# Layer 1 of a four-layer graph network: rows of the neighbours scaled ahead of the loop, GpSimd's product over both chunks of a pair in one instruction, and the last rows stored through three queues

## The chip, the cores and the metric

The kernel runs on one core of a Trainium2 chip. Its time is device microseconds (us) of one execution; the time before is 559.01 us, the median of three runs from 558.31 to 559.95 us. A core has five engines that run their own instruction streams in order and wait for each other through semaphores: TensorE (PE in the profile, with its weight loads as PEld), VectorE (DVE), ScalarE (ACT), GpSimd (POOL) and SyncE (SP), which here only starts transfers. SP, ACT and POOL can start DMA transfers.

## The reference, cut to what matters

Four graph layers, each followed by a residual and a layer norm, work on x (3327 nodes by 64 features) and one dense matrix adj (3327 by 3327). The change is in layer 1, a hyperbolic attention layer, and in the stores of the last layer.

```python
x_tan = _logmap0(x, C)
left = x_tan @ att_W[:D] + att_b
right = x_tan @ att_W[D:]
adj_att = jax.nn.sigmoid(left + right.T) * adj
x_local = _logmap(x[:, None, :], x[None, :, :], C)
support_t = jnp.einsum('ij,ijd->id', adj_att, x_local)
return _proj(_expmap(x, support_t, C), C)
...
x = _layernorm(x + _L1_gnn_ref(x, adj, L1_gnn_att_W, L1_gnn_att_b), axis=-1)
```

For every pair of nodes (i, j) layer 1 needs a sigmoid times adj, and a logarithmic map of the two points. After the layer norm of layer 0 all rows have nearly the same norm, and the kernel replaces the map's scalar factor by a cubic polynomial in one inner product of i and j. The cubic is evaluated as a linear (real) factor times a quadratic factor.

## The kernel before

Nodes are padded to 3328 = 26 blocks of 128. In layer 1 (`near_sphere`) the 128 partitions hold neighbours j of one block, and the free axis holds nodes i. The work is cut into 104 tiles `(cp, jb, ci)`: two column halves cp, 26 blocks jb, and two chunks ci. A tile is 128 partitions by 2 x 416 = 832 elements. Two tiles with the same cp and jb form a pair (here pair k has the tiles 2k and 2k + 1); they share one slab of adj and one sigmoid of 1664 elements.

For a tile t the program issues:

- `products(t)` (L1099), PE: the inner products of j and i into a PSUM tile pq; three such tiles exist, so the products of t + 3 wait for the last reader of t.
- `attention(k)` (L1065 to L1088), once for a pair: SP loads adj, ACT computes sg = sigmoid(lb + rb) over 1664 elements (L1075), and GpSimd multiplies it by adj, u = sg * at (L1086), in two instructions of 832 elements, one for each tile. There are two buffers of sg and four of u. For pair 0 the sigmoid is cut in two as well.
- `linear(t)` (L1105): DVE computes a = (pq + dl) * u (L1111), where dl is one number for each partition j, and then ACT squares in place, pq = (gas * pq + al)^2 (L1112).
- `gather(t)` (L1116): DVE computes v = (pq + constant) * a (L1120), and PE adds xv(j)^T v to the accumulators (L1132).

All engines of this stage follow an order written out by hand (`manual_schedule`). The loop over t is `linear(t + 1)`, `gather(t)`, and, at even t, `attention(t // 2 + 2)` and, in the first half, `rows_of_sums` (L1226, a small ACT instruction). From this follow the orders on the engines:

- DVE: a(t+1), v(t), a(t+2), v(t+1), ...
- ACT: for t = 2k: square(t+1), sigmoid of pair k + 2, rows_of_sums, square(t+2), square(t+3), ...
- POOL: u(0), u(1), u(2), ...

At t = 13 and t = 25 PE also turns two more groups of blocks, and ACT copies them out of PSUM ahead of its next sigmoid.

Ahead of the loop DVE writes the rows of i into ri (`rows_of_i`, L1218; these rows carry -2 * gas) and the last columns of ri and xv, GpSimd computes dl and al (L1255 to L1257), and PE turns ri and lj. lj holds rows of j: 63 differences of features and in the last column (aa + 1) * inv_s (L1007). Here s is the layer norm's scale of a row, inv_s its inverse, ga another number of a row, and gas = ga * s.

After the loop, `near_end` works on 128 x 26 statistics (k, gp, ps and so on, L1464 to L1568), rebuilds the layer's output with `x2 = alpha * m + beta * xc` and the like, and layer 2 begins at L419.

The last layer's second half ends in `last_out`. DVE scales three parts of the output, in the order blocks 10 to 12, 6 to 9, 0 to 5, and each part is stored when it is ready. Block 12 has only 127 real rows, which go by themselves through ACT's queue (L848); the others go through SP (10 and 11), ACT (6 to 9) and SP (0 to 5).

Of the kernel before, what the change touches and what calls it, by code (L numbers as in the profile page):

```python
# [10 lines left out]
F32 = mybir.dt.float32  # L11
# [49 lines left out]
CUBIC_ROOT = -1.39229596292  # L61
CUBIC_SHIFT = 0.0453813261445
CUBIC_REST = 1.75705840270866
NEIGH = 100
# [10 lines left out]
def kernel(  # L75
# [234 lines left out]
    def layers(ctx, x2, x3, begun_here, kept, ready, ahead_ctx, strm):  # L310
# [496 lines left out]
        def last_out(h, accT):  # L807
# [33 lines left out]

            for s, queue in zip(parts[::-1], (nc.sync, nc.scalar, nc.sync)):
                nc.vector.scalar_tensor_tensor(
                    hh[:, s], hh[:, s], -0.5, spread(r[:, s], s.stop - s.start),
                    op0=ALU.mult, op1=ALU.mult,
                )
                if s.stop == NBH:
                    nc.scalar.dma_start(out[N - rows :], hh[:rows, NBH - 1])  # L848
                store(queue, h, hh, s)
# [45 lines left out]
    with tc.tile_pool(name="l1", bufs=1) as l1:  # L895
# [20 lines left out]
        with tc.tile_pool(name="l1a", bufs=1) as l1a, tc.tile_pool(  # L916
# [86 lines left out]
            vec(ga, vq[:, 1], rq[:, 1], ALU.mult)  # L1003
            stt(inv_s, vq[:, 1], -0.5 / 0.9, r2[:, 1], op0=ALU.mult, op1=ALU.mult)
            sca(aa, g1, -1.0, 1.0, ALU.mult, ALU.add)
            vec(gas, ga, s, ALU.mult)
            stt(lj[:, :, D - 1], aa, 1.0, inv_s, op0=ALU.add, op1=ALU.mult)  # L1007
        in_order.close()

        def near_sphere(mT, ljT_0, xm, sq_e, t_e, rows_63):  # L1010
# [3 lines left out]
            with tc.tile_pool(name="n1", bufs=1, reuse_waits="tile") as n1, tc.tile_pool(  # L1014
# [50 lines left out]
                def attention(pair):  # L1065

                    if pair >= len(tiles) // 2:
                        return
                    cp, jb, _ = tiles[2 * pair]
                    at, sl = load(cp, jb), slot(jb)  # L1070
                    sg = n1w.tile([P, 2, 2 * CW], F32, tag="sg", name=f"sg_{pair}")
                    lbs = lbh[:, :, cp * 2 * CW : (cp + 1) * 2 * CW]

                    def sigmoid(of):
                        nc.scalar.activation(  # L1075
                            sg[:, :, of], lbs[:, :, of], AF.Sigmoid, bias=rb[:, sl : sl + 1]
                        )

                    chunks = (slice(0, CW), slice(CW, 2 * CW))
                    if pair:  # L1080
                        sigmoid(slice(0, 2 * CW))
                    for ci, of in enumerate(chunks):
                        if not pair:
                            sigmoid(of)
                        u = n1w.tile(TW, F32, tag="u", bufs=4, name=f"u_{pair}_{ci}")
                        nc.gpsimd.tensor_tensor(u, sg[:, :, of], at[:, :, of], ALU.mult)  # L1086
                        us[2 * pair + ci] = u
                        yield  # L1088
# [16 lines left out]
                def linear(t):  # L1105

                    if t >= len(tiles):
                        return
                    one = slice(slot(tiles[t][1]), slot(tiles[t][1]) + 1)
                    a_s[t] = n1w.tile(TW, F32, tag="a", bufs=3, name=f"a_{t}")  # L1110
                    stt(a_s[t], pqs[t], dl[:, one], us.pop(t), op0=ALU.add, op1=ALU.mult)  # L1111
                    nc.scalar.activation(  # L1112
                        pqs[t], pqs[t], AF.Square, bias=al[:, one], scale=gas[:, one]
                    )
# [109 lines left out]
                def rows_of_sums(jb):  # L1224
                    sl = slot(jb)
                    nc.scalar.activation(  # L1226
                        xv[:, sl, : D - 1], xc[:, sl, : D - 1], AF.Copy, scale=xf[:, sl : sl + 1]
                    )
# [12 lines left out]
                with tc.manual_schedule(  # L1241
# [6 lines left out]
                    keep((NB - 3, NB - 4))  # L1248
                    stt(xf, gas, CUBIC_LEAD / -256.0, gas, op0=ALU.mult, op1=ALU.mult)
                    nc.vector.tensor_copy(ri[:, :, D - 1], ga)  # L1250
                    vec(xv[:, :, D - 1], lj[:, :, D - 1], xf, ALU.mult)
                    rows_of_i(0, 4)
                    rows_of_i(4, NBH)

                    nc.gpsimd.tensor_scalar(dl, g1, CUBIC_ROOT, -1.0, ALU.mult, ALU.add)  # L1255
                    nc.gpsimd.tensor_tensor(dl, dl, inv_s, ALU.mult)
                    nc.gpsimd.tensor_scalar(al, ga, -1.0, CUBIC_SHIFT, ALU.mult, ALU.add)  # L1257
                    spread_a, spread_b = bank(0, left, 0, 4), bank(1, left, 13, 4)
# [30 lines left out]
                    for t in range(len(tiles)):  # L1289
# [13 lines left out]
                        if t == len(tiles) - 4:  # L1303
                            of = slice(0, 2 * CW)
                            nc.gpsimd.tensor_tensor(xm[:, of], mT[:, of], ljT[0][:, of], ALU.mult)
# [3 lines left out]
                            gp.tensor_tensor(gk, gs, ga, ALU.mult)  # L1309
# [14 lines left out]
                        if t == len(tiles) - 2:  # L1324
# [5 lines left out]
                                t_e.rearrange("p (a k h) -> p a k h", a=2, k=3), pm[..., P:]  # L1330
                            )
                    stt(rxn, r2[:, 0], -0.5, inv_s, op0=ALU.mult, op1=ALU.mult)
                    vec(xn, aa, rxn, ALU.mult)

        def near_end(mT, ljT, xm, sq_e, t_e, rows_63, x2):
# [4 lines left out]
            with tc.tile_pool(name="l1e", bufs=1) as l1e, tc.tile_pool(  # L1340
# [78 lines left out]

                gt, q, k, ps = st("gt"), st("q"), st("k"), st("ps")  # L1420
                gp = st("gp")
# [42 lines left out]
                vec(k, p, gks, mul)  # L1464
                vec(gp, p, gss, mul)
                vec(k, k, gt, add)
                vec(ps, p, s, mul)

# [49 lines left out]
                vec(be, be, ck, sub)  # L1518
                alp = of(mul, al, ps, "alp")
                al2 = of(mul, al, al, "al2")  # L1520
# [45 lines left out]
                alpha, beta = dl, xf  # L1566
                stt(alpha, n_r, -0.5, al, op0=mul, op1=mul)
                stt(beta, n_r, -0.5, be, op0=mul, op1=mul)  # L1568

                for b, g, n in ((0, 0, 1), (0, 1, 3), (3, 12, 1), (1, 4, 4), (2, 8, 4)):  # L1570
# [4 lines left out]
                    vec(lj[:, sl], lj[:, sl], one(beta, sl), mul)  # L1575
                    vec(lj[:, sl], lj[:, sl], pt, add)

                for g, n in threes:
                    sl = slots(g, n)
                    vec(x2[:, sl], x2[:, sl], one(alpha, sl), mul)  # L1580
                    vec(xc[:, sl], xc[:, sl], one(beta, sl), mul)
                    vec(x2[:, sl], x2[:, sl], xc[:, sl], add)
# [270 lines left out]
```

## Time and profile before

| what | us |
|---|---|
| median of three runs | 559.01 |
| the profiled execution | 559.12 |
| its span, from the first to the last instruction | 557.4 |
| from the first a (L1111) to the end of the last v (L1120) of layer 1 | 22.22 to 227.68 |
| layer 2's first matmul (L419) | 243.0 |
| the last DVE instruction ends | 550.1 |
| busy: PE, DVE, ACT, POOL | 525.1, 377.8, 276.2, 215.5 |

The profile is of one execution. Its span runs from the first to the last instruction. The timeline gives for each instruction the start and the duration in us, the engine, the line of the kernel, the output and inputs by their names, and in brackets the idle time in front of it with what ended it. Consecutive instructions of the same line are merged with their number behind an x. DVE and ACT start an instruction a little before the one ahead of it has ended, so the step from start to start is shorter than a duration.

```profile
PE   7889989999999999999999999999999999999991
PEld 5522222222222222764444444444455555545541
DVE  6899999999999999899000010300578877887733
ACT  4799999999999998530000100000364333433321
POOL 3699999999999999300000000000001000000000
PEclk9899999999999999899999999999999999999996
DMA  8977776766676717799999039999019994799601
```

These are the busy tenths of 40 equal slices of 13.9 us. In the slices from 22 to 220 us, layer 1's loop, four engines are busy nearly all of the time.

### The profile page before, as it was taken

The page shows a single profiled execution, that of the slowest core. Times are in us where ns is not written, and L with a number is a line of the kernel's source. Part 1 is how long each engine was busy: PE and PEld are TensorE (multiplying, and loading weights), DVE is VectorE, ACT ScalarE, POOL GpSimd, SP SyncE. Part 2 cuts the span into 40 slices and gives each one's busy share as a digit, 9 for nine tenths or more (in the row PEclk, how much of TensorE's full clock was granted, in tenths as well). Part 3 has the DMA queues.
Part 4 walks back from the last instruction along what each step waited for, and adds up shares of the span by engine and source line. Part 5 has one row for each costly group of instructions (what it writes and reads, how often), then busy time and mean ns, then how long its engine had stood idle before and what let it go on. Part 6 is the DMA issues. An engine that isn't in the chain of part 4 may idle for free.

```text
span 557.4 us, 7490 instructions
## 1 busy us (share of the span) xinstructions
PE 525.1 (94%) x2841; PEld 226.5 (41%) x2841; DVE 377.8 (68%) x547; ACT 276.2 (50%) x323; POOL 215.5 (39%) x138
## 2 busy tenths in 40 slices
PE   7889989999999999999999999999999999999991
PEld 5522222222222222764444444444455555545541
DVE  6899999999999999899000010300578877887733
ACT  4799999999999998530000100000364333433321
POOL 3699999999999999300000000000001000000000
PEclk9899999999999999899999999999999999999996
DMA  8977776766676717799999039999019994799601
GB/s 287 357 254 232 209 229 201 224 210 227 206 237 211 220 60 272 294 427 425 422 423 418 16 141 422 420 426 413 15 55 328 342 327 177 244 270 362 257 1 37
DMA packets 33893, 143.57 MB, mean 258 GB/s; under 512 B 10269, under 2 KB 11959, under 8 KB 28855
## 3 DMA queue, kind: packets, MB, share of 16 engines
q1 hardware_dynamic: 31511, 142.40, 69.9%
q10 hardware_dynamic: 2336, 0.59, 0.5%
q8 instruction: 24, 0.39, 0.3%
q14 instruction: 22, 0.18, 0.1%
HBM read 141.53 MB, written 0.87 MB: 255 GB/s over the span
## 4 chain that ended last, share of the span: by engine, by line
PE 66%; DVE 20%; ACT 8%; issue 3%; DMA 1%; DVEq 0%
PE cnt L419 25%; PE pq L1099 12%; DVE v L1120 12%; PE cnt L524 11%; PE acc L720 6%; ACT sg L1075 4%; PE acc L735 3%; ACT pq L1112 3%; DVE a L1111 2%; DVE w L537 1%; PE cnt L410 1%; DVE mask L339 1%; DMA x<-in_x 1%; PE x_w L1435 1%; PE pn_l L371 1%
## 5 line engine op out<-in xcount | busy, mean ns | idle before, releaser
L1086 POOL TENSOR_TENSOR u<-sg,at 128x832 f32<-128x832 f32 x88 | 169.9, 1959 | 3.5 <-ACT sg L1075 3.1
L1099 PE MATMUL pq<-riT,ljT 64*128 64x416 f32 x416 | 100.2, 560 | 15.2 <-DVE v L1120 6.2
L1111 DVE SCALAR_TENSOR_TENSOR a<-pq,dl,u 128x832 f32<-128x832 f32 x104 | 112.1, 1078 | 2.9 <-PE pq L1099 2.8
L1112 ACT ACTIVATE pq<-pq,al,gas 128x832 f32<-128x832 f32 x104 | 105.0, 1011 | 15.2 <-DVE a L1111 14.3
L1120 DVE SCALAR_TENSOR_TENSOR v<-pq,a 128x832 f32<-128x832 f32 x104 | 105.8, 1017 | 1.1 <-ACT pq L1112 0.7
L1132 PE MATMUL acc<-v,xv 128*64 128x416 f32 x416 | 95.4, 537 | 0.1
L1075 ACT ACTIVATE sg<-lb,rb 128x1664 f32<-128x1664 f32 (+1 forms) x53 | 87.3, 1647 | 0.1
L539 ACT ACTIVATE w<-cnt 128x832 int16<-128x832 f32 x55 | 47.2, 863 | 71.5 <-PE cnt L524 71.4
L419 PE MATMUL cnt<-at_l,lj 128*64 128x416 f32 x448 | 80.2, 513 | 0.0
L651 POOL TENSOR_TENSOR s<-sq,s 128x384 bf16<-128x384 f32 (+1 forms) x4 | 4.1, 1026 | 195.0 <-ACT s L650 195.0
L504 ACT ACTIVATE x<-cnt 128x416 f32<-128x416 f32 x8 | 4.1, 517 | 130.6 <-PE cnt L419 130.6
L1099 PEld LDWEIGHTS pq<-riT,ljT 64*128 64x128 f32 x416 | 31.5, 184 | 88.3 <-DVE v L1120 83.0
L537 DVE TENSOR_SCALAR w<-cnt 128x832 int16<-128x832 f32 x49 | 50.2, 1024 | 25.2 <-PE cnt L524 23.8
L524 PE MATMUL cnt<-mask,tri 128*128 128x416 bf16 x208 | 53.5, 339 | 0.1
L720 PE MATMUL acc<-w,s 128*128 128x416 bf16 x208 | 52.6, 339 | 0.5 <-DVE hid L792 0.5
L524 PE MATMUL cnt<-mask,rest 128*128 128x416 bf16 x200 | 51.6, 340 | 1.2 <-ACT w L539 0.6
L419 PEld LDWEIGHTS cnt<-at_l,lj 128*64 128x64 f32 x448 | 31.9, 137 | 46.0 <-issue 45.2
L1132 PEld LDWEIGHTS acc<-v,xv 128*64 128x64 f32 x416 | 20.6, 134 | 61.0 <-issue 57.8
L339 DVE TENSOR_SCALAR mask<-ah 128x1664 bf16<-128x1664 f32 x42 | 43.4, 1034 | 0.5 <-DMA ah<-in_adjT 0.5
L407 DVE COPY lj<-pn_l 128x512 f32<-128x512 f32 (+1 forms) x4 | 2.4, 592 | 60.9 <-PE pn_l L371 60.9
L419 PE MATMUL cnt<-kept,lj 128*64 128x416 f32 x224 | 41.2, 513 | 0.0
L1086 POOL TENSOR_TENSOR u<-sg,kept 128x832 f32<-128x832 f32 x16 | 31.0, 1959 | 3.6 <-ACT sg L1075 3.6
(286 smaller groups left out, 411.7 us busy)
## 6 DMA issues: line engine op xcount, KB each, us to landing
at_l<-in_adjT SPq DMA_DIRECT2D x24, 1664.0 KB, 13.2
at<-in_adjT SPq DMA_DIRECT2D x44, 832.0 KB, 5.0
ah<-in_adjT SPq DMA_DIRECT2D x42, 832.0 KB, 6.5
bt_l<-in_adjT SPq DMA_DIRECT2D x8, 1664.0 KB, 16.8
kept<-in_adjT SPq DMA_DIRECT2D x7, 1664.0 KB, 9.2
lb<-lf_rows SPq DMA_DIRECT2D x2, 384.0 KB, 4.3
ljT<-ljT SPq DMA_DIRECT2D x4, 128.0 KB, 5.2
x<-in_x ACTq DMA_DIRECT2D x1, 416.0 KB, 5.3
```

The lines of the kernel that those rows point to most:

```text
L339: nc.vector.tensor_scalar(mask[q], at, 0.0, None, ALU.not_equal)
L419: nc.tensor.matmul(acc[c][h * D : (h + 1) * D, :], hw[:, slot(jb), :], blocks[jb][:, o : o + CW], start=c not in begun, stop=last, skip_gr ...
L524: nc.tensor.matmul(cnt[c][:, e, :], mat, mask[q][:, of], start=start, stop=(mat is tri), skip_group_check=True,)
L537: nc.vector.tensor_scalar(w.bitcast(I16), cnt[c], 0.0, None, ALU.max)
L720: nc.tensor.matmul(acc[h, c][:, e, :], s12[:, slot(jb)].rearrange("p t d -> p (t d)"), ws[q, c][:, e, :], start=first, stop=last,)
L1075: nc.scalar.activation(sg[:, :, of], lbs[:, :, of], AF.Sigmoid, bias=rb[:, sl : sl + 1])
L1086: nc.gpsimd.tensor_tensor(u, sg[:, :, of], at[:, :, of], ALU.mult)
L1099: nc.tensor.matmul(pq[:, h, :], ljT[h != jb // NBH][rows, of], riT[rows, ch * CW : (ch + 1) * CW], start=True, stop=True,)
L1111: stt(a_s[t], pqs[t], dl[:, one], us.pop(t), op0=ALU.add, op1=ALU.mult)
L1112: nc.scalar.activation(pqs[t], pqs[t], AF.Square, bias=al[:, one], scale=gas[:, one])
L1120: stt(w, pqs.pop(t), CUBIC_REST, a_s.pop(t), op0=ALU.add, op1=ALU.mult)
L1132: nc.tensor.matmul(accs[cp, ci][h * D : (h + 1) * D, :], xv[:, slot(jb), :], w[:, h, :], start=(jb == orders[cp][0]), stop=(jb == orders[c ...
```

## The change

Three edits are made.

1. lj's 63 features and its last column are scaled by s, so that pq comes out scaled by s of its row j. The last column becomes aa + 1, the real factor's shift becomes the same constant for all j (`CUBIC_PLUS`), an immediate in L1111 in place of the column dl, and the square's scale becomes ga. The scaling is done ahead of the loop by three DVE multiplications (`scaled`), `rows_of_i` is cut into three instead of two, dl is no longer computed, inv_s is computed behind the loop, and some 128 x 26 statistics of `near_end` change or fall away.
2. The product sg * adj is written in place over sg, of which there are three buffers now; the four buffers of u fall away. For pairs 0 and 1 it is still made in two instructions; from pair 2 on, one instruction covers the 1664 elements of both chunks.
3. In `last_out` the 127 rows of block 12 are split into 112, through ACT's queue, and 15, through POOL's; blocks 6 to 9 go through SP and blocks 0 to 5 through ACT.

The order of instructions on PE and ACT is the same as before, the operands and the stores aside.

```diff
+CUBIC_PLUS = 2 * CUBIC_ROOT - 1
...
-            for s, queue in zip(parts[::-1], (nc.sync, nc.scalar, nc.sync)):
+            most = rows // 16 * 16
+            for s, queue in zip(parts[::-1], (nc.sync, nc.sync, nc.scalar)):
...
                 if s.stop == NBH:
-                    nc.scalar.dma_start(out[N - rows :], hh[:rows, NBH - 1])
+                    nc.scalar.dma_start(out[N - rows : N - rows + most], hh[:most, NBH - 1])
+                    nc.gpsimd.dma_start(out[N - rows + most :], hh[most:rows, NBH - 1])
                 store(queue, h, hh, s)
...
-            stt(inv_s, vq[:, 1], -0.5 / 0.9, r2[:, 1], op0=ALU.mult, op1=ALU.mult)
...
-            stt(lj[:, :, D - 1], aa, 1.0, inv_s, op0=ALU.add, op1=ALU.mult)
+            sca(lj[:, :, D - 1], aa, 1.0, None, ALU.add)
...
-                    sg = n1w.tile([P, 2, 2 * CW], F32, tag="sg", name=f"sg_{pair}")
+                    sg = n1w.tile([P, 2, 2 * CW], F32, tag="sg", bufs=3, name=f"sg_{pair}")
...
-                    for ci, of in enumerate(chunks):
+
+                    wide = slice(0, 2 * CW)
+                    for of in chunks if pair < 2 else (wide,):
                         if not pair:
                             sigmoid(of)
-                        u = n1w.tile(TW, F32, tag="u", bufs=4, name=f"u_{pair}_{ci}")
-                        nc.gpsimd.tensor_tensor(u, sg[:, :, of], at[:, :, of], ALU.mult)
-                        us[2 * pair + ci] = u
+                        nc.gpsimd.tensor_tensor(sg[:, :, of], sg[:, :, of], at[:, :, of], ALU.mult)
+                        for ci, c in enumerate(chunks):
+                            if of in (c, wide):
+                                us[2 * pair + ci] = sg[:, :, c]
                         yield
...
-                    stt(a_s[t], pqs[t], dl[:, one], us.pop(t), op0=ALU.add, op1=ALU.mult)
+                    stt(a_s[t], pqs[t], CUBIC_PLUS, us.pop(t), op0=ALU.add, op1=ALU.mult)
                     nc.scalar.activation(
-                        pqs[t], pqs[t], AF.Square, bias=al[:, one], scale=gas[:, one]
+                        pqs[t], pqs[t], AF.Square, bias=al[:, one], scale=ga[:, one]
                     )
...
-                    stt(xf, gas, CUBIC_LEAD / -256.0, gas, op0=ALU.mult, op1=ALU.mult)
-                    nc.vector.tensor_copy(ri[:, :, D - 1], ga)
+                    def scaled(b, n):
+
+                        sl = slice(2 * b, 2 * (b + n))
+                        vec(
+                            lj[:, sl, : D - 1], lj[:, sl, : D - 1],
+                            s[:, sl].unsqueeze(2).to_broadcast([P, 2 * n, D - 1]), ALU.mult,
+                        )
+
+                    scaled(9, 4)
+                    sca(ri[:, :, D - 1], ga, -CUBIC_ROOT, None, ALU.add)
+                    rows_of_i(0, 4)
+                    stt(xf, ga, CUBIC_LEAD / -256.0, ga, op0=ALU.mult, op1=ALU.mult)
                     vec(xv[:, :, D - 1], lj[:, :, D - 1], xf, ALU.mult)
-                    rows_of_i(0, 4)
-                    rows_of_i(4, NBH)
-
-                    nc.gpsimd.tensor_scalar(dl, g1, CUBIC_ROOT, -1.0, ALU.mult, ALU.add)
-                    nc.gpsimd.tensor_tensor(dl, dl, inv_s, ALU.mult)
-                    nc.gpsimd.tensor_scalar(al, ga, -1.0, CUBIC_SHIFT, ALU.mult, ALU.add)
+                    vec(gss, xf, s, ALU.mult)
+                    rows_of_i(4, 8)
+                    scaled(5, 4)
+                    rows_of_i(8, NBH)
+                    scaled(0, 5)
+
+                    nc.gpsimd.tensor_scalar(
+                        al, ga, CUBIC_PLUS, CUBIC_SHIFT - CUBIC_ROOT, ALU.mult, ALU.add
+                    )
...
-                            gp.tensor_tensor(gss, gs, s, ALU.mult)
-                            gp.tensor_tensor(gks, gk, s, ALU.mult)
-                            gp.tensor_scalar(gks, gks, -2.0, None, ALU.mult)
+                            gp.tensor_scalar(gks, gk, -2.0, None, ALU.mult)
...
+                    stt(inv_s, vq[:, 1], -0.5 / 0.9, r2[:, 1], op0=ALU.mult, op1=ALU.mult)
                     stt(rxn, r2[:, 0], -0.5, inv_s, op0=ALU.mult, op1=ALU.mult)
...
-                vec(ps, p, s, mul)
...
-                vec(be, be, s, mul)
...
+                vec(beta_c, beta, s, mul)
```

More of the change, by code (lines that the diff above doesn't have):

```diff
@@ L1226, in rows_of_sums @@
                     nc.scalar.activation(
-                        xv[:, sl, : D - 1], xc[:, sl, : D - 1], AF.Copy, scale=xf[:, sl : sl + 1]
+                        xv[:, sl, : D - 1], xc[:, sl, : D - 1], AF.Copy, scale=gss[:, sl : sl + 1]
                     )
@@ L1418, in p_of @@
                         )
-                gt, q, k, ps = st("gt"), st("q"), st("k"), st("ps")
+                gt, q, k = st("gt"), st("q"), st("k")
                 gp = st("gp")
@@ L1464, in near_end @@
                 vec(k, p, gks, mul)
-                vec(gp, p, gss, mul)
+                vec(gp, p, gs, mul)
                 vec(k, k, gt, add)
-                vec(ps, p, s, mul)
                 first = in_bank("first_w")
@@ L1518, in near_end @@
                 vec(be, be, ck, sub)
-                alp = of(mul, al, ps, "alp")
+                alp = of(mul, al, p, "alp")
                 al2 = of(mul, al, al, "al2")
@@ L1565, in near_end @@
                 stt(n_r, n_r, -3.0, t, op0=add, op1=mul)
-                alpha, beta = dl, xf
+                alpha, beta, beta_c = dl, xf, gss
                 stt(alpha, n_r, -0.5, al, op0=mul, op1=mul)
@@ L1580, in near_end @@
                     vec(x2[:, sl], x2[:, sl], one(alpha, sl), mul)
-                    vec(xc[:, sl], xc[:, sl], one(beta, sl), mul)
+                    vec(xc[:, sl], xc[:, sl], one(beta_c, sl), mul)
                     vec(x2[:, sl], x2[:, sl], xc[:, sl], add)
```

## The prediction

> **What bounds the kernel now.** I read the 40 slices first, then the busy time of each engine in two stretches of layer 1's loop (columns: window and length, then for PE, PEld, DVE, ACT and POOL the busy us and the number of instructions, then clock, DMA share and GB/s):
>
> ```profile
> 100.00:150.00 50.00, 46.55 (x208) 12.76 (x204) 49.75 (x52) 47.16 (x48) 49.42 (x27) 1.00 0.68 216
> 150.00:200.00 50.00, 47.05 (x210) 12.97 (x208) 50.00 (x53) 45.57 (x40) 49.99 (x27) 1.00 0.67 217
> ```
>
> DVE and POOL are both full, at the same rate, 26 tiles in 50 us. That is too neat for two engines that merely happen to be busy, so I read the timeline for what releases what (lines of DVE, ACT and POOL, by engine; counting the a instructions, the a at 166.54 is tile 73's):
>
> ```profile
> 166.54 1.08 DVE L1111 SCALAR_TENSOR_TENSOR a<-pq,dl,u 128x832 f32<-128x832 f32 x1
> 167.54 1.01 DVE L1120 SCALAR_TENSOR_TENSOR v<-pq,a 128x832 f32<-128x832 f32 x1
> ...
> 172.34 1.08 DVE L1111 SCALAR_TENSOR_TENSOR a<-pq,dl,u 128x832 f32<-128x832 f32 x1
> 173.34 1.01 DVE L1120 SCALAR_TENSOR_TENSOR v<-pq,a 128x832 f32<-128x832 f32 x1
> 174.28 1.08 DVE L1111 SCALAR_TENSOR_TENSOR a<-pq,dl,u 128x832 f32<-128x832 f32 x1
> ...
> 167.66 1.02 ACT L1112 ACTIVATE pq<-pq,al,gas 128x832 f32<-128x832 f32 x1 [0.34 <-DVE a L1111]
> 168.60 1.67 ACT L1075 ACTIVATE sg<-lb,rb 128x1664 f32<-128x1664 f32 x1
> ...
> 168.39 3.92 POOL L1086 TENSOR_TENSOR u<-sg,at 128x832 f32<-128x832 f32 x2
> ```
>
> The a of tile 73 ends at 167.62; its square starts 0.04 later; the sigmoid of tiles 76 and 77 stands behind that square on ACT and starts 0.94 after it; it ends at 170.27. Of the two products in the last line the second, tile 76's, starts at 170.35 (3.92 less one of 1.96), 0.08 after the sigmoid, and ends at 172.31. Tile 76's a starts 0.03 later, then v, then tile 77's a at 174.28. So there is a closed round, a(73) to a(77): 1.08 + 0.04 + 0.94 + 1.67 + 0.08 + 1.96 + 0.03 + 1.00 + 0.94 = 7.74 us for two pairs, with no slack in any link. DVE alone needs 2 x 2 x (1.00 + 0.94) = 7.76, POOL 4 x 1.93 = 7.72. Three limits coincide within 0.04 us. The waits table names few waits because a tie leaves no idle time to name; only the release times show the round.
>
> **Part 1, the constant and the scaled rows.** The rows that price it, and the product's (line, engine, operation, shapes, count, then busy us and mean ns):
>
> ```profile
> L1111 DVE SCALAR_TENSOR_TENSOR a<-pq,dl,u 128x832 f32<-128x832 f32 x104 | 112.1, 1078 | 2.9 <-PE pq L1099 2.8
> L1120 DVE SCALAR_TENSOR_TENSOR v<-pq,a 128x832 f32<-128x832 f32 x104 | 105.8, 1017 | 1.1 <-ACT pq L1112 0.7 <-PE pq_early L1320 0.2
> L537 DVE TENSOR_SCALAR w<-cnt 128x832 int16<-128x832 f32 x49 | 50.2, 1024 | 25.2 <-PE cnt L524 23.8 <-ACT xc L639 1.0
> L751 DVE TENSOR_SCALAR x<-acc,b_sb 128x832 f32<-128x832 f32 x2 | 2.2, 1084 | 5.5 <-PE acc L720 5.5
> ...
> L1305 POOL TENSOR_TENSOR x<-mT,ljT 128x832 f32<-128x832 f32 x1 | 1.9, 1940 | 0.0
> L651 POOL TENSOR_TENSOR s<-sq,s 128x512 bf16<-128x512 f32 x1 | 1.2, 1152 | 6.9 <-ACT s L650 6.9
> L1309 POOL TENSOR_TENSOR gk<-gs,ga 128x26 f32<-128x26 f32 x1 | 0.2, 239 | 0.1
> ```
>
> The a with a column operand takes 61 ns more than v with an immediate; L751 against L537 shows the same 60 ns. So a falls to 1.02 us and to a step of 0.93: DVE needs 1.86 instead of 1.94 us a tile, 0.15 us a pair. This counts only if DVE sets the pace.
>
> Ahead of the loop DVE gets three multiplications of 504, 504 and 630 elements. The 512-element L1576 takes 0.69 us, so about 0.68 + 0.68 + 0.83; a third rows_of_i and three small operations add 0.3. Of these 2.5 us DVE's waits for PE (0.6 at 18.8 us, 0.9 at 20.1) cover most: the last copy of riT, which now starts at 21.03, I place at 22.3, and PE's pq with it at about 22.1 instead of 21.1. I take +1.0 us at the first a; bounds 0 (all covered) and 2.5 (nothing covered). After the loop, L1467 and L1562 leave the DVE chain (0.1 each): -0.2. The moved inv_s (0.17) lies in DVE's 0.79 us wait for PE before L1443, and beta_c (0.12) ahead of x2's rows, which nothing waits for yet; without this cover they would cost 0.3.
>
> **Part 2, one product for two tiles.** It removes 50 POOL instructions, and lengthens a link of the round: tile 76's a now waits for the product of both chunks. Queued behind it on DVE are v of the tile before and the next a; behind these stand that a's square and the sigmoid of two pairs later. The third sg buffer does not help: the sigmoid is held by its place behind the square on ACT, and that order is unchanged; it does not wait for a buffer.
>
> The duration P of a 1664-element product is not in the trace. From 832 and 26 elements, same operation and types: (1.957 - 0.239) / 806 = 2.13 ns an element, so P = 1.957 + 832 x 0.00213 = 3.73; from L1305's 1.940 it is 3.70. Upper bound: two products as now, 3.92. Lower bound: if the fixed part is as in L651 and L940 (512 elements 1.152, 819 elements 1.553, so 1.31 ns each and 0.48 fixed), P = 0.48 + 1664 x (1.957 - 0.48) / 832 = 3.43. I take 3.70, by the row with the same types.
>
> The new round: 1.02 + 0.04 + 0.94 + 1.67 + 0.08 + 3.70 + 0.03 + 0.93 + 0.94 = 9.35 us for two pairs, 4.68 a pair against 3.87. DVE (3.72), POOL (3.70) and ACT (about 3.7 with rows_of_sums) have slack under it, so no other limit joins.
>
> The sum over the loop: two rounds interlock, one through the odd tiles 1, 5, 9 ..., one through 3, 7, 11 ... I follow the second to the end. The sigmoid of tiles 4 and 5 (26.09 now) starts at 27.1 by the +1.0; it ends at 28.8, product to 32.5. The product of tiles 6 and 7 follows directly, to 36.2; a(6) 36.26, a(7) 38.13 (35.63 now). From a(7) to a(103) are 24 rounds: 224.4, so 262.5. ACT's copies at t = 13 and 25 delay a sigmoid of just this round, by 2 x 0.59 and 2 x 0.28 = 1.7: a(103) starts at 264.3 against 224.50 now. That is **+39.8 us** (+1.0 of it from part 1). What follows a(103) keeps its length, 3.2 us to the end of the last v; layer 2 begins that much later, and its adj is prefetched in time as now.
>
> **Part 3, the stores.** The DMA answers of three successive us, 552 to 555:
>
> ```profile
> DMA packets 769, 0.21 MB, mean 213 GB/s; under 512 B 766, under 2 KB 766, under 8 KB 766
> ...
> DMA packets 89, 0.02 MB, mean 22 GB/s; under 512 B 89, under 2 KB 89, under 8 KB 89
> ...
> DMA packets 33, 0.02 MB, mean 24 GB/s; under 512 B 31, under 2 KB 31, under 8 KB 31
> ```
>
> From 553 on only a tenth of the rate is left: a single-file tail of 256-byte packets until 554.8, after which the program ends at 557.4. At the full rate the last 120 packets would take 0.16 us, so spreading gains at most 1.5. Against it: no transfer on POOL's queue is in this trace, and if it took the longest issue to landing of any output store here, 7.6 us, from 549.3, it would end 2.1 us after 554.8. I take -1.0: a typical store lands after 4.4 to 5.3, inside the others' time.
> Two rules of the Trainium skill disagree here. DMA: Bandwidth & Descriptors, section Issuing engines are not separate DMA queues, says that all queues share 16 DMA engines and another queue saves only issue time; by it the part is worth 0, the sum 598.7. The same page, section Why a DMA increments its semaphore by 16 and not by 1, says that 127 rows go through one DMA engine and 112 through 16; by that the tail goes, as I priced it from the rows.
>
> **The sum.** Against the profiled execution's 559.12 (0.1 above the median 559.01): 559.12 + 39.8 - 0.2 - 1.0 = **597.7 us**.
>
> **Rivals.**
> (a) Faster: the round does not bind, because products of 1664 are short or come early enough. Then 25 pairs gain 0.15 (DVE), 24 in the first half about 0.07 (ACT's 3.7 with its waits): 559.12 - 5.4 - 1.0 = 552.7. For it: DVE is full and really gets faster. Against it: the round without P is 5.65, DVE's two pairs are 2 x 3.72, so it decides only if P is under 7.44 - 5.65 = 1.8 us, less than one product of 832 takes today.
> (b) Slower yet: PE works 3.8 us of each pair's 3.87 now and 3.8 of 4.68 then; if its granted clock fell to half for the loop, as between 234 and 237 us (0.58 in 233.5 to 236), its 16 matmuls a pair (0.175 each in L419's unbroken run of 272 in 47.64) would go from 2.8 to 5.6 us and set the pace: 50 x (5.6 - 4.68) = 46 more, 644. Against it: PE would still work 0.81 of the time, and every window of the loop today shows 1.00.
> (c) The change does not do what it says: POOL's wide product lets a start on its first half. Then POOL's rate (3.70) rules and it is (a). The new order shows the first a of a pair waiting for POOL's instruction, which has one end.
>
> **How the numbers follow.** Forecast 0.90, (a) with (c) 0.05, (b) 0.03, no measurable change 0.02. P moves the time by 24 us per us: 3.43 gives -6.5, 3.92 gives +5.3; the start adds -1 to +1.5, the stores -0.5 to +3.1, the copies up to -1.7. Not all at once: 589 to 604. Chances of over 0.3% faster 0.05, within 0.3% (1.7 us, what a measurement of this kernel can tell from none) 0.02, slower 0.93.
>
> **What would show it.** Right: pairs 4.6 to 4.8 us apart, DVE waiting about 1 us at the even a for POOL, POOL waiting for the sigmoid, products of 3.4 to 3.9, a at 1.02, no single-file tail. Wrong: if DVE is full through the loop or ACT's sigmoids run ahead of the squares.

## The result and the profile after

The changed kernel takes 604.05 us, the median of four runs (602.83 to 604.76), against 559.48 us (558.31 to 560.66) for the kernel before on the same chip: a ratio of 1.080, with a 95% interval from 1.0785 to 1.0816. It is slower, as forecast, by the mechanism that was forecast; but the median lies 6.35 us above the 597.7 and just outside the range, which ended at 604.0. The profiled execution took 604.45 us, its span is 602.6 us.

In the new line numbers a is L1117, the square L1118, v L1126, the sigmoid L1078, GpSimd's product L1090, `rows_of_i` L1224 and `scaled` L1258. First the two stretches of the loop that were shown of before (columns: window, length, busy us and instructions of PE, PEld, DVE, ACT and POOL, then clock, DMA share, GB/s):

```profile
100.00:150.00 50.00, 38.42 (x172) 10.60 (x172) 41.21 (x44) 40.48 (x43) 39.44 (x12) 1.00 0.57 180
150.00:200.00 50.00, 38.97 (x172) 10.54 (x172) 40.01 (x43) 39.17 (x34) 39.41 (x12) 1.00 0.56 180
```

No engine is full any more: DVE and POOL went from some 50 to 40 us of 50, and the TensorE clock is still 1.00. Work that waits while all engines have spare time is the mark of a closed chain. The three groups of the round (the last part of a line is the idle time ahead of the group and what ended it):

```profile
L1090 POOL TENSOR_TENSOR sg<-sg,at 128x1664 f32<-128x1664 f32 x44 | 163.8, 3722 | 44.5 <-ACT sg L1078 42.3
...
L1117 DVE SCALAR_TENSOR_TENSOR a<-pq,sg 128x832 f32<-128x832 f32 x104 | 106.0, 1020 | 46.8 <-POOL sg L1090 44.5
L1118 ACT ACTIVATE pq<-pq,al,ga 128x832 f32<-128x832 f32 x104 | 105.5, 1015 | 58.8 <-DVE a L1117 58.6
```

They wait in a ring: POOL for the sigmoid, a for POOL, the square for a. Before, a's group had 2.9 us of idle time and now has 46.8. One turn of it in the timeline (start, duration, engine, line):

```profile
106.67 1.01 DVE L1117 SCALAR_TENSOR_TENSOR a<-pq,sg 128x832 f32<-128x832 f32 x1
107.60 1.01 DVE L1126 SCALAR_TENSOR_TENSOR v<-pq,a 128x832 f32<-128x832 f32 x1
...
114.15 1.02 DVE L1117 SCALAR_TENSOR_TENSOR a<-pq,sg 128x832 f32<-128x832 f32 x1 [0.85 <-POOL sg L1090]
115.09 1.01 DVE L1126 SCALAR_TENSOR_TENSOR v<-pq,a 128x832 f32<-128x832 f32 x1
116.03 1.02 DVE L1117 SCALAR_TENSOR_TENSOR a<-pq,sg 128x832 f32<-128x832 f32 x1
...
107.71 1.02 ACT L1118 ACTIVATE pq<-pq,al,ga 128x832 f32<-128x832 f32 x1 [0.84 <-DVE a L1117]
108.66 1.67 ACT L1078 ACTIVATE sg<-lb,rb 128x1664 f32<-128x1664 f32 x1
...
110.40 3.72 POOL L1090 TENSOR_TENSOR sg<-sg,at 128x1664 f32<-128x1664 f32 x1 [0.96 <-ACT sg L1078]
```

The a at 106.67 releases its square at 107.71, behind it on ACT stands the sigmoid at 108.66, the product starts 0.07 after it and ends at 114.12, the even a of that pair starts at 114.15, and the odd one at 116.03: 9.36 us for two pairs, where the prediction had 9.35.

So the loop is as forecast. The start is not (the timeline again, of the stretch ahead of the loop):

```profile
17.22 0.68 DVE L1224 SCALAR_TENSOR_TENSOR mT<-xc,gas 128x504 f32<-128x504 f32 x1
17.81 2.46 DVE L1258 TENSOR_TENSOR lj<-lj,s 128x504 f32<-128x504 f32 x1
20.19 2.55 DVE L1224 SCALAR_TENSOR_TENSOR mT<-xc,gas 128x630 f32<-128x630 f32 x1
22.66 2.54 DVE L1258 TENSOR_TENSOR lj<-lj,s 128x630 f32<-128x630 f32 x1
...
28.42 1.02 DVE L1117 SCALAR_TENSOR_TENSOR a<-pq,sg 128x832 f32<-128x832 f32 x1 [1.42 <-PE pq L1105]
...
17.76 9.24 POOL L1090 TENSOR_TENSOR sg<-sg,kept 128x832 f32<-128x832 f32 x4 [2.16 <-ACT sg L1078]
...
26.55 3.15 PE L1105 MATMUL pq<-riT,ljT 64*128 64x416 f32 x8 [6.56 <-DVE riT L1216]
```

The same operation on 504 elements takes 0.68 us at 17.22 and 2.46 us at 17.81, when POOL has begun its products. The three long ones lie on POOL's first three products one by one: those end at 19.73, 22.07 and 24.53, and the DVE operations at 20.27, 22.74 and 25.20. DVE counts as busy all that time; a group's busy time doesn't tell that it waits. PE, which waits for DVE's copy of riT, stands idle for 6.56 us, and then works at half speed: its eight matmuls take 3.15 us at a granted clock of 0.50, where before they took 1.67 at 1.00:

```profile
21.09 1.67 PE L1099 MATMUL pq<-riT,ljT 64*128 64x416 f32 x8
```

So the first a waits 1.42 us for PE where it waited 0.50 before; 0.9 us of the late start is the clock.

The spans, cut at the same events (us of the profiled executions; the predicted column comes from the prediction's own sum):

| stretch | before | predicted | after |
|---|---|---|---|
| start of the first a | 22.22 | 23.2 | 28.42 |
| start of tile 7's a | 35.63 | 38.13 | 44.42 |
| a(7) to a(103), 24 rounds | 188.87 | 226.1 | 226.17 |
| a(103) to the end of the last v | 3.18 | 3.2 | 3.13 |
| to layer 2's first matmul | 15.33 | 15.1 | 15.37 |
| to the end of DVE's last instruction | 307.06 | 307.1 | 307.06 |
| to the end of the span | 7.31 | 6.3 | 6.48 |

Nearly the whole miss, 6.3 us, is in place when a(7) starts. These are single executions: in five runs that have the start of the kernel before, the first a came between 20.98 and 22.32 us, so a difference of one us there says little. For the stores, the three DMA answers of before are set against those for 598 to 601 us here, a stretch that begins 1.8 us after DVE's end (1.9 before):

```profile
DMA packets 435, 0.12 MB, mean 123 GB/s; under 512 B 433, under 2 KB 433, under 8 KB 433
...
DMA packets 2, 0.02 MB, mean 16 GB/s; under 512 B 0, under 2 KB 0, under 8 KB 0
...
DMA packets 1, 0.01 MB, mean 8 GB/s; under 512 B 0, under 2 KB 0, under 8 KB 0
```

The single-file tail is gone (769, 89 and 33 packets before; the last three here aren't output, being larger than its 256 bytes): the last packet of data lands 2.5 us after DVE's end instead of 4.4. The span's end came nearer by only 0.82.

### The profile page after: what moved, and what is told of

The parts are those of the page before. It is cut to its first block, busy times and chain, and to the rows that moved or that the text cites. A ratio compares the mean times of both kernels' runs of the same rounds, so it can differ in the third digit from the quotient of the medians.

```text
span 602.6 us, 7394 instructions
## 1 busy us (share of the span) xinstructions
PE 527.4 (88%) x2841; PEld 226.1 (38%) x2841; DVE 381.8 (63%) x551; ACT 279.2 (46%) x323; POOL 209.7 (35%) x85
## 4 chain that ended last, share of the span: by engine, by line
POOL 32%; PE 32%; issue 30%; DVE 3%; ACT 2%; DMA 1%; POOLq 0%; DVEq 0%; ACTq 0%
POOL sg L1090 31%; PE cnt L421 24%; PE cnt L526 1%; PE cnt L412 1%; DMA x<-in_x 1%; PE pm L1409 1%; PE x_w L1453 1%; PE pn_l L373 1%; PE both L593 1%; DVE a L1117 1%; PE m_w L1453 1%; PE pe L1433 0%; PE acc L722 0%; ACT w L541 0%; ACT sg L1078 0%
## 5 line engine op out<-in xcount | busy, mean ns | idle before, releaser
L1090 POOL TENSOR_TENSOR sg<-sg,at 128x1664 f32<-128x1664 f32 x44 | 163.8, 3722 | 44.5 <-ACT sg L1078 42.3
L1105 PE MATMUL pq<-riT,ljT 64*128 64x416 f32 x416 | 102.6, 572 | 56.6 <-DVE v L1126 47.9
L1117 DVE SCALAR_TENSOR_TENSOR a<-pq,sg 128x832 f32<-128x832 f32 x104 | 106.0, 1020 | 46.8 <-POOL sg L1090 44.5
L1118 ACT ACTIVATE pq<-pq,al,ga 128x832 f32<-128x832 f32 x104 | 105.5, 1015 | 58.8 <-DVE a L1117 58.6
L1126 DVE SCALAR_TENSOR_TENSOR v<-pq,a 128x832 f32<-128x832 f32 x104 | 105.5, 1015 | 1.1 <-ACT pq L1118 0.8
L1078 ACT ACTIVATE sg<-lb,rb 128x1664 f32<-128x1664 f32 (+1 forms) x53 | 87.3, 1647 | 0.1
## 6 DMA issues: line engine op xcount, KB each, us to landing
bt_l<-in_adjT SPq DMA_DIRECT2D x8, 1664.0 KB, 15.4
```

Of the source, the lines that this page charges most:

```text
L1078: nc.scalar.activation(sg[:, :, of], lbs[:, :, of], AF.Sigmoid, bias=rb[:, sl : sl + 1])
L1090: nc.gpsimd.tensor_tensor(sg[:, :, of], sg[:, :, of], at[:, :, of], ALU.mult)
L1105: nc.tensor.matmul(pq[:, h, :], ljT[h != jb // NBH][rows, of], riT[rows, ch * CW : (ch + 1) * CW], start=True, stop=True,)
L1117: stt(a_s[t], pqs[t], CUBIC_PLUS, us.pop(t), op0=ALU.add, op1=ALU.mult)
L1118: nc.scalar.activation(pqs[t], pqs[t], AF.Square, bias=al[:, one], scale=ga[:, one])
L1126: stt(w, pqs.pop(t), CUBIC_REST, a_s.pop(t), op0=ALU.add, op1=ALU.mult)
```

## The experiments

Ratios are to the kernel before on the same chip, with 95% intervals. "Rounds" are a(7) to a(103).

**The width of the product.** One run takes it back out of the change, the other makes it alone:

```diff
-                    for of in chunks if pair < 2 else (wide,):
+                    for of in chunks:
```

> The changed kernel with one edit undone: every pair's product in two instructions of 832 again, still in place over three sg buffers. Round theory: the round is 1.02 + 0.04 + 0.94 + 1.67 + 0.08 + 1.96 + 0.03 + 0.93 + 0.94 = 7.61 us, so a(7) to a(103) takes 24 x 7.61 and some 3.5 of stalls at t = 13, 25 and the change of halves, about 186 instead of 226, and the time falls by 40 to about 564. Rival (the product in place, or the constant, slows the loop, and not the width): the time stays above 595.

Measured: 562.12 us, 1.0057 [1.0038, 1.0077]; rounds 187.1 us.

> The kernel before with the second edit alone: product in place, three sg buffers, one instruction of 1664 from pair 2 on; no constant, no scaled rows, stores as before. Round theory: 1.08 + 0.04 + 0.94 + 1.67 + 0.08 + 3.72 + 0.03 + 1.00 + 0.94 = 9.50 us a round, a(7) to a(103) about 229, a(7) some 2 late, so 559 + 40 + 2 = about 601; the first a stays at 22.2. Rival (half of the loss comes from the other edits): under 585.

Measured: 602.02 us, 1.0748 [1.0719, 1.0777]; rounds 229.7 us, with the first a at 22.32 as in the kernel before. The two runs bracket the part: without it the loop is that of before, with it alone the loss is nearly whole. They also show part 1 within the loop: 229.7 less 226.2 is 3.5 us. Of this 0.7 is one round of e2 (47.0 to 57.1 us, 10.17 us) in which the granted TensorE clock was 0.83; the medians of the 24 rounds are 9.49 and 9.37, so the shorter a, which stands in two links of a round, brings 0.12 in each. In e1 part 1 brings only 1.8 us: POOL's two halves, 3.84 us a pair from start to start, then take longer than DVE's 3.72.

**Part 1 alone** (the kernel before with the scaled rows and the constant, products in halves):

> The kernel before with the first edit alone: constant and scaled rows; product in two halves into u, stores as before. Theory of contention: DVE's scaling and rows_of_i run against GpSimd's first products and take about 2.5 us instead of 0.7 to 0.9, so the first a is at about 28.4 and the time is about 559 + 6 to 8 for the start, less 3 for the shorter round: 562 to 564. Rival (DVE merely has 2.5 us more to do, and the late start came from the wide products): first a at 23 to 24, time about 557.

Measured: 562.71 us, 1.0058 [1.0032, 1.0084]; rounds 187.3, first a at 26.34. That is 2.1 earlier than expected and tells more than the expected figure would have. Its timeline has a hole between POOL's first two products:

```profile
17.48 2.44 DVE L1254 TENSOR_TENSOR lj<-lj,s 128x504 f32<-128x504 f32 x1
19.84 0.80 DVE L1220 SCALAR_TENSOR_TENSOR mT<-xc,gas 128x630 f32<-128x630 f32 x1
20.56 2.56 DVE L1254 TENSOR_TENSOR lj<-lj,s 128x630 f32<-128x630 f32 x1
...
17.32 2.05 POOL L1088 TENSOR_TENSOR u<-sg,kept 128x832 f32<-128x832 f32 x1 [2.06 <-ACT sg L1076]
19.94 2.51 POOL L1088 TENSOR_TENSOR u<-sg,kept 128x832 f32<-128x832 f32 x1 [0.56 <-ACT sg L1076]
```

`rows_of_i` of 630 elements starts at 19.84, when POOL is idle, and takes 0.80, where the changed kernel's took 2.55; now the product behind it is the late one, 2.51 instead of 1.95. Whoever starts second stands still.

The run with two halves (e1) has the very start of the changed kernel, since pairs 0 and 1 are halved in both, and yet its first a came at 25.98 instead of 28.42:

```profile
17.91 0.68 DVE L1258 TENSOR_TENSOR lj<-lj,s 128x504 f32<-128x504 f32 x1
18.51 2.57 DVE L1224 SCALAR_TENSOR_TENSOR mT<-xc,gas 128x630 f32<-128x630 f32 x1
...
18.38 8.88 POOL L1090 TENSOR_TENSOR sg<-sg,kept 128x832 f32<-128x832 f32 x4 [2.68 <-ACT sg L1078]
```

Its first product started at 18.38 instead of 17.76, behind the multiplication at 17.91, which took 0.68; two operations were held instead of three, and PE's matmuls behind them took 1.67 us at a clock of 1.00, so that the first a waited 0.63 instead of 1.42. So the loss at the start of one and the same code was 3.8 us in one execution and 6.2 in another: some 1.7 of the difference by which engine came first, 0.8 by the clock. What lowers the clock isn't shown: it was 1.00 in e1 after PE had been idle for 3.53 us, and 0.50 in e3 after 3.09.

**What kind of DVE operation is held.** Both runs put all rows of i first and the two later multiplications of lj last, in one case by 18 operations with one SBUF tensor and a column each, in the other by two with two SBUF tensors:

```diff
                     vec(gss, xf, s, ALU.mult)
-                    rows_of_i(4, 8)
-                    scaled(5, 4)
-                    rows_of_i(8, NBH)
-                    scaled(0, 5)
+                    rows_of_i(4, NBH)
+                    for k in range(18):
+                        sca(lj[:, k, : D - 1], lj[:, k, : D - 1], s[:, k : k + 1], None, ALU.mult)
```

> The changed kernel with rows_of_i written before the second and third scaling, and these two cut into 18 operations of 63 elements, each with one tensor input and a column as the scalar. Theory: a DVE operation with two SBUF inputs waits until GpSimd's running product has ended, one with a single input doesn't; so these take about 0.11 each, 2.0 together, and the first a comes at 23 to 24 instead of 28.4; time about 599 to 600. Rival (any DVE work beside GpSimd's product is stretched): first a after 27.

Measured: 608.05 us, 1.0869 [1.0838, 1.0900]; first a at 31.65. The expectation fell: the 18 operations took 9.87 us. The timeline, in two windows, shows it (the last field is the number of operations):

```profile
18.56 1.95 DVE L1271 TENSOR_SCALAR lj<-lj,s 128x63 f32<-128x63 f32 x1
...
24.85 3.58 DVE L1271 TENSOR_SCALAR lj<-lj,s 128x63 f32<-128x63 f32 x11
...
18.37 4.01 POOL L1090 TENSOR_TENSOR sg<-sg,kept 128x832 f32<-128x832 f32 x2 [2.68 <-ACT sg L1078]
22.95 3.83 POOL L1090 TENSOR_TENSOR sg<-sg,kept 128x832 f32<-128x832 f32 x2 [0.57 <-ACT sg L1078]
```

One such operation of 63 elements takes 1.95 us beside POOL's first product. Of the last eleven the first takes 1.97, until the last product ends at 26.78, and the other ten 0.24 each, 0.16 from start to start. So the one-tensor form is held as well, one operation for each whole product; many small ones only make it worse. The a and v have one operand in PSUM, and take 1.02 and 1.01 us beside products all through the loop. The Trainium skill (SBUF — State Buffer, section Who interferes with whom) has this as a rule: VectorE and GpSimd share a pair of SBUF ports under an exclusive lock; a VectorE instruction with two SBUF inputs contends for it with a GpSimd one that reads SBUF, and so does one in a mode that uses two ports, which plain tensor_scalar can enter; the second to issue stands fully blocked. The times here agree with it: 0.68 to 2.46 and 0.24 to 1.95 us on the one side, 1.97 to 2.5 us for a product on the other. That the 63-element form ran in that mode isn't visible in a trace.

> As the run with one input, in the same order, but the second and third scaling as in the changed kernel, one operation of two SBUF inputs each. Theory: each waits for a product and takes 2.0 to 2.6 us instead of 0.7 to 0.8; first a at 26 to 27, 3 us after that of the run with one input. Rival (the order was the matter, not the inputs): first a within 0.5 us of that run's.

Measured: 603.99 us, 1.0807 [1.0770, 1.0845]; first a at 26.71, as expected: two operations are held instead of three, 4.92 us together. The time is no better than the changed kernel's: a(7) starts 2.35 us earlier, but the rounds took 227.6 instead of 226.2. The difference lies in two rounds, the first and the seventh, of 10.17 and 9.96 us, in which the granted clock fell. Here is the first with the one behind it (columns as above, the clock third from the end):

```profile
42.07:52.24 10.17, 8.12 (x32) 2.25 (x32) 7.82 (x10) 8.40 (x10) 8.22 (x3) 0.83 0.41 123
52.24:61.61 9.37, 7.90 (x36) 2.04 (x34) 7.63 (x8) 7.61 (x9) 7.45 (x3) 1.00 0.48 158
```

**The wait taken away.** If the cause is the overlap, it goes when GpSimd starts later. A copy of one column out of the last scaled rows stands ahead of its first product (on top of the order of the run before):

```diff
+                    held = n1w.tile([P, 1], F32, tag="held", bufs=1, name="held")
+                    nc.gpsimd.tensor_copy(held, lj[:, 0, 0:1])
                     start = attention(0)
```

> The changed kernel with the order of two_inputs (rows_of_i 4 to 12, then scaled(5, 4) and scaled(0, 5) with two inputs), and one GpSimd copy of a single column out of the rows that scaled(0, 5) writes, ahead of GpSimd's first product, so that the products start only when the scaling is done. Theory (DVE operations with all operands in SBUF stand still while a GpSimd product runs): the two multiplications take 0.68 and 0.8 us instead of 4.92 together, all four first products take 1.95 to 2.0, the first a starts near 23.7 us (26.7 in two_inputs, 28.4 in the changed kernel), and the time is about 601 us, 3 less than two_inputs and as much over the 597.7 predicted as the later first products cost; the loop's 24 rounds stay at 226 us. Rival (the multiplications are slow by their own shape or by ScalarE's or the transfers' use of the memory): they take 4.9 together again, and the first a comes later than 26.7.

Measured: 599.26 us, 1.0712 [1.0685, 1.0740]; first a at 22.27, a(7) at 37.51, rounds 226.9. The timeline:

```profile
18.35 1.40 DVE L1258 TENSOR_TENSOR lj<-lj,s 128x504 f32<-128x504 f32 x2
...
22.27 1.02 DVE L1117 SCALAR_TENSOR_TENSOR a<-pq,sg 128x832 f32<-128x832 f32 x1 [0.48 <-PE pq L1105]
...
20.04 7.71 POOL L1090 TENSOR_TENSOR sg<-sg,kept 128x832 f32<-128x832 f32 x4
```

The two multiplications take 1.40 us together instead of 4.92, and the four products 7.71 instead of 9.58, though nothing was taken out: GpSimd starts 2.4 us later and the loop starts 4.4 us sooner (e10, below, has the same start, and its first a came at 23.63, 3.1 sooner). Of the 4.4, 3.5 are DVE's, and 0.9 is PE's clock, 0.50 in the run before and 1.00 here. The rivals are out. The shape is the same. ScalarE and the transfers don't do it either: here ScalarE is busy for 1.21 of the 1.40 us, at a DMA share of 0.92; in the changed kernel it is idle throughout the last multiplication (22.66 to 25.20, DMA share 0.95), which took 2.54 us for 630 elements. With the contention gone, a(7) starts at 37.5, where the prediction had 38.13, and the time comes within 1.6 us of 597.7.

**The stores.**

```diff
-                    nc.gpsimd.dma_start(out[N - rows + most :], hh[most:rows, NBH - 1])
+                    nc.scalar.dma_start(out[N - rows + most :], hh[most:rows, NBH - 1])
```

> The kernel before with the third edit alone: 112 rows through ACT's queue, 15 through POOL's, blocks 6 to 9 through SP, 0 to 5 through ACT. Theory: the single-file tail goes, the last output packet lands about 2.5 us after DVE's end instead of 4.4, but the program's end takes 1 us longer; net 0.8 to 0.9 us faster, ratio about 0.9985. Rival (other queues share the same DMA engines and save nothing): ratio 1.000 and the tail stays.

Measured: 558.99 us, 0.9985 [0.9971, 1.0000].

> As the run with the stores alone, but the 15 rows go through ACT's queue too, behind the 112, so that POOL's queue isn't used. If POOL's queue costs the extra 1 us at the program's end, this is 1.5 to 2 us faster than before, less up to 0.4 for one more issue on ACT; if the end has another cause, it is no faster than the run with three queues.

Measured: 557.67 us, 0.9973 [0.9959, 0.9987]. In the profiled executions the last data packet lands 2.64 us after DVE's end with three queues and 2.78 with two (4.37 before), but the span ends 7.39 and 6.36 us after it (7.31 before). That looks as if GpSimd's queue cost 1 us at the program's end, but the other profiles don't bear it out: with GpSimd's queue the span ends 6.48 (the changed kernel) to 7.45 us after DVE in seven of them, with two queues 6.36 to 6.80 in three, with the stores of before 7.31 to 7.71 in three. What all ten with split rows have in common is a longer way from the last data packet to the span's end, 3.6 to 4.7 us instead of 2.9 to 3.3; part of the gain is lost there, whichever queue carries the 15 rows. The intervals of the two runs overlap, so a cost of GpSimd's queue isn't shown.

**The round opened.** The sigmoid and product are issued three pairs ahead, with four buffers; the wide product stays:

```diff
-                    sg = n1w.tile([P, 2, 2 * CW], F32, tag="sg", bufs=3, name=f"sg_{pair}")
+                    sg = n1w.tile([P, 2, 2 * CW], F32, tag="sg", bufs=4, name=f"sg_{pair}")
...
                     list(attention(1))
+                    list(attention(2))
...
-                            list(attention(t // 2 + 2))
+                            list(attention(t // 2 + 3))
```

> The changed kernel with the sigmoid and product of a pair issued three pairs ahead instead of two, and four sg buffers; the wide product stays. Round theory: the round of 9.4 us then spans three pairs (3.1 a pair) and binds no more; DVE's 3.72 a pair does, and about 3.8 in the first half where ACT has its extra instruction: a(7) to a(103) about 24 x 3.80 + 24 x 3.73 + 3.5 = 184 instead of 226, so about 562. Rival (the wide product as such is what GpSimd or its port can't sustain): over 590.

Measured: 559.64 us, 1.0004 [0.9984, 1.0023]; rounds 184.0 us, as expected. The same stretch by engine:

```profile
150.00:200.00 50.00, 48.85 (x216) 13.22 (x214) 50.00 (x55) 47.35 (x41) 50.00 (x15) 1.00 0.68 220
```

DVE and POOL are both full again, with the product at 3.74 us and the late start still in. So the wide product costs its 39 us (226.2 less the 187.1 of e1) only through its place in the round, and the earlier issue gives 42 back; as work for GpSimd it is cheaper than two halves (3.74 us against 3.92).

**What beats the kernel before.** Three pairs ahead, the held start and the stores through two queues:

> The changed kernel with three parts of the earlier runs together: the sigmoid and product three pairs ahead with four buffers, the held start of the run before, and the stores through two queues without GpSimd's. Theory: the savings add, as they lie at different places: 559.6 of three_ahead, less some 4.7 at the start (first a near 23.7 instead of 28.4), less some 0.8 at the end: about 554 us, ratio to the kernel before 0.991, and below every version so far. a(7) to a(103) stays at 184 us. Rival: the start's saving is lost again on GpSimd, whose first products start 2.4 us later and which has 12 us of products in front of a(7): then 556 to 557.

Measured: 555.93 us (554.98 to 557.61), 0.9925 [0.9906, 0.9944]: the fastest version here, 2 us short of the sum. a(7) starts at 37.98, 4.0 earlier than with three ahead alone, and the rounds keep 184.0 us, so the start's saving isn't lost on GpSimd. The 0.8 us expected at the end isn't seen: the span ends 6.62 us after DVE, in e5 6.52. The profile is that of its longest run, 557.61; there 16.8 us instead of 15.4 lie between the last v and layer 2, where TensorE's granted clock is 0.50 for 4 us. What the other executions lack of the sum stays open.

> The kernel before with the wide product three pairs ahead (four buffers) and the stores through two queues, but without part 1: lj isn't scaled, the a keeps its column dl. This tells what part 1 is worth once the round no longer binds. Theory (DVE then sets the pace with 1.94 us a tile instead of GpSimd and DVE with 1.87): first a at 22.3 us and a(7) at about 36, a(7) to a(103) 187.5 us (184.0 in the run with part 1), the end as in two_queues: about 557 to 558 us, ratio to the kernel before 0.997; part 1 is then worth some 1.5 us net of its held start. Rival (part 1 brings nothing beside its start): a(7) to a(103) 184 us and the time 553 to 554.

Measured: 559.51 us, 1.0009 [0.9991, 1.0027]; first a at 21.12, rounds 188.2 us.

```profile
150.00:200.00 50.00, 47.28 (x210) 12.97 (x208) 50.00 (x53) 45.79 (x40) 48.59 (x14) 1.00 0.60 195
```

DVE is full and POOL has 1.4 us to spare: without part 1 DVE sets the pace, with an a of 1.073 us. So part 1 is worth 4.2 us of rounds once the round is open; the times of the two runs differ by 3.6. Parts 1 and 2 each made the kernel slower alone (e3, e2); what gained 0.75% is both with the earlier issue, the held start and the stores, which alone bring 0.27% (e8). Part 1 with the earlier issue and the held start, but with the product in halves, wasn't run, so it isn't shown that the wide product is needed for the gain.

## Why the prediction was right and where it failed

- **The round and its length.** Right: 9.36 us against 9.35, P 3.72 against 3.70, 226.17 us for 24 rounds with ACT's copies against 226.1. e2 shows that the width makes it alone, e5 that issuing the sigmoid and product one pair earlier ends it. The bounds of P, 3.43 and 3.92, were wider than needed: the row with the same operation and types was the right one.
- **a's 1.02 us.** Right (1.020); e12 and e10 show what it is worth.
- **The start: the step that failed.** "I take +1.0 us at the first a; bounds 0 (all covered) and 2.5 (nothing covered)" measured +6.2 (+3.8 in e1, which has the same start). The durations, 0.68 and 0.83 us, came from rows in which GpSimd didn't run. The bounds allowed for where DVE's added work lies, not for its getting longer beside another engine's work. Moving it to after 17.8 us laid it over GpSimd's products; three operations were held about 1.8 us each, and 0.9 us came on top by PE's clock, which the prediction had left at full speed. In the trace of before these operations end at 18.20 and GpSimd's first product starts at 18.50, so no row of that stretch shows them together; that the two lie 0.3 us apart was there to be read:

```profile
16.19 2.01 DVE L1218 SCALAR_TENSOR_TENSOR mT<-xc,gas 128x504 f32<-128x504 f32 x2
...
18.50 3.98 POOL L1086 TENSOR_TENSOR u<-sg,kept 128x832 f32<-128x832 f32 x2 [2.07 <-ACT sg L1075]
```

Elsewhere the trace of before does show such a wait. Of its 42 operations of L339 the median takes 1.02 us and one takes 1.72, the only one that starts while GpSimd multiplies:

```profile
412.87 1.72 DVE L339 TENSOR_SCALAR mask<-ah 128x1664 bf16<-128x1664 f32 x1
...
412.79 0.91 POOL L651 TENSOR_TENSOR s<-sq,s 128x384 bf16<-128x384 f32 x1 [8.62 <-ACT s L650]
```

e3, e6 and e9 show the cause.
- **From the first a to a(7).** A further 1.1 us beyond that (16.0 where the sum had 14.9): the products pq of tile 7 took 1.67 us instead of 0.97, in a stretch with a granted clock of 0.64. e2, e7 and e9, where the clock was 1.00 in the last 3 us before a(7), took 15.2 to 15.4, and e6, where it was 0.58, 15.8; so some 0.7 goes with the clock. Not tried separately.
- **After the loop.** -0.2 was predicted, 0.04 more was measured: what was taken out there didn't show.
- **The stores.** -1.0 predicted, -0.82 in the changed kernel's profile, though alone they brought 0.15% with an interval that ends at no change. The direction was right, the reason incomplete: the tail shrank by 1.8 us, more than the 1.5 allowed for it, and part came back behind it, which the sum didn't have; that the net came out near -1.0 is partly luck.
- **The range.** It held every term but the start, whose upper bound was 3.7 us too low, and the 1.1 us behind it, which had none. With the measured +6.2 in place of +1.0 the sum is 602.9, and a bound that took the overlap in would have carried the range beyond 607. With the +3.8 of e1 the sum would be 600.5, inside the range, though beyond the start's own bound.
- **The rivals.** (a) and (c), the round doesn't bind: out, by the ring of waits. With the round opened the time was 559.64 in e5 and 555.93 in e10, which also has the held start; (a) had 552.7, without a late start. (b), the clock: 1.00 in the loop's windows. It did fall to 0.83 over single rounds of e2, e7 and e9, at a cost of 0.6 to 0.8 us each, far from the 46 of (b).

## What to carry to other kernels

When engines have spare time and yet wait for each other in a ring, count the links of the ring: a longer instruction in one link costs its whole added length in every turn, even if it saves work on its engine, and issuing the next turn's work one place earlier gives it back. A duration from a row holds only beside the same neighbours: before moving VectorE work that reads two tensors from SBUF, or a tensor_scalar from SBUF to SBUF, see whether GpSimd computes at that time, and if so let one wait for the other on purpose. Edits can be worth something only together: try the parts singly and joined.

## What the runs showed of the hardware

- A VectorE operation with two tensors in SBUF, or a tensor_scalar from SBUF to SBUF, and a GpSimd product of two SBUF tensors didn't run at once. A held one shows as a long one, never as idle time. They took turns, one instruction each: 2.4 to 2.6 us for operations of 0.7 to 0.8, 1.95 for one of 0.24, and 2.5 for products of 1.95. GpSimd's product of 832 elements was held too when VectorE was first (2.51 in e3). Not every VectorE operation in SBUF is held: of two reductions of 832 elements in the changed kernel (5.59 to 7.54 us) the second started in the midst of GpSimd's product of 819 elements (5.64 to 7.19) and took 1.01 us, the first 1.02.
- Starting GpSimd 2.4 us later made the whole stretch 4.4 us shorter (e9 against e7, one execution each; 3.1 by e10), 0.9 of it by the granted clock of the matmuls behind.
- With the last 127 rows in one store the last output packet landed 4.33 to 4.38 us after DVE's end (three profiles), with 112 and 15 rows 2.54 to 2.88 us (ten profiles), with or without GpSimd's queue.
- In single rounds of the loop the granted TensorE clock fell to 0.83 (e2, e7, e9) and the round took 0.6 to 0.8 us more; in e7 that makes up the whole difference of 1.4 us to the changed kernel's rounds. One more such round in e7 and one in e9, at 0.82, took no longer than in the changed kernel (9.71). Ahead of the loop it was 0.50 in the changed kernel, e3 and e7, and eight matmuls took 3.14 to 3.15 us instead of 1.67.
